# Strassen's products for the two-tile passes of a mixture-of-experts layer, and a second bank for the sums of its second matrix

## The chip, the cores and the metric

The kernel runs on one core of a Trainium2 chip, in fp32 throughout. The time is that of one execution on the device, in microseconds. In the profile PE is the engine of the matmuls, PEld its loading of weights, DVE the vector engine, ACT the scalar engine, POOL the GpSimd engine and SP the engine whose queue issues most of the DMAs.

## The reference

Two sequences of 1024 tokens of 512 numbers go through a feed-forward layer, an attention layer and a second feed-forward layer with the same weights, each added to its input. The attention (16 heads, with 64 memory slots and gates) isn't touched by the change. The feed-forward layer sends each token to one of two experts:

```python
logits = x_flat @ w_router.T
probs = softmax(logits); top_idx = argmax(probs); top_weight = probs[top_idx]
h = einsum('nd,ehd->enh', x_flat, w_fc)          # 512 -> 2048
a = square(where(h >= 0, h, 0.5 * h))
expert_out = einsum('enh,edh->end', a, w_proj)   # 2048 -> 512
out = einsum('end,en->nd', expert_out, mask * top_weight)
x = x + 0.5 * ffn(layernorm(x))
```

## The kernel before

A feed-forward layer (`ffn`, called once for each) sorts the tokens by expert and works them off in six passes; a pass is one, two or four tiles of 128 tokens that all go through one expert. The first layer's passes (FIRST) have 2, 4, 2, 4, 1 and 4 tiles, the last layer's (LAST) 4, 4, 4, 2, 2 and 1. Pass 0 of the first layer is cut up to begin while tokens still arrive. A pass takes the 2048 hidden units in four chunks (`ck`) of 512. Each chunk needs 1 MB of the first matrix (wfc) and 1 MB of the second (wp), loaded on SP's queue into a ring of 11 large buffers. "Pass 2_1" below means pass 2, chunk 1.

*Plain chunks* (passes of one and two tiles): `hidden` (L514) multiplies, four matmuls for each of four blocks of 128 hidden units, with all tokens of the pass as moving columns (128 or 256). `activate` (L496) does the leaky square: ACT takes a scaled ReLU of the product in PSUM (L500), DVE combines it with the product in PSUM (L501), ACT squares. `project` (L733) multiplies by wp, four matmuls of 512 columns for each tile, and its sums stay in PSUM over the four chunks; after the last one DVE scales them by the router's weight and adds the input (L740), and `send` (L653) scatters the tile with an indirect DMA on POOL's queue.

*Fast chunks* (passes of four tiles): both matrix products are done as Strassen's, in Winograd's form, with seven products of half-sized blocks in place of eight.

- Sums of blocks come first. Of the tokens: `token_sums`, four DVE operations for each pass (L538-544). Of the weights: `weight_sums` (S, L553-557) and `output_sums` (R, L567-571), eight POOL operations for each chunk, into a ring of six buffers (`sums`). Of the activations: `unit_sums` (Q, L588-591), eight DVE operations for each chunk.
- `hidden_fast` (L598-645) runs twice in a chunk (q = 0, 1), with 14 matmuls each (L611) into three banks, hU, hV and hC. DVE and ACT put the products together into hA and hB in SBUF: hA from hC (L627), hB from hV (L636), ACT copies (L618, L639), hA from hV (L643). hV gets its second product only after hB has been taken from its first. `activate` then reads hA and hB in SBUF (L503), and ACT squares.
- `project_fast` (L664) runs its products between the hidden matmuls of the next chunk, three at each step. Three of the seven (`keep`) gather in banks of their own over the four chunks; the other four (`add`) go through a bank of tag "at", of which `keep` leaves one free, and are added into osum in SBUF, by ACT in chunk 0 (L692) and by DVE after it (L694).
- `finish_fast` (L706-723) puts the output blocks together on DVE in the next pass's chunk 0, scales them (L721) and sends the tiles.

`prepare` (L476-493) normalises the next pass's tokens on DVE (xn, L481) and transposes them on PE through the bank "tr" (`lt`, L487). All engines take their instructions in program order, and so do the queues of SP and POOL.

The attention's weights need such sums too. `Attention.weight_sums` (L858-905) makes those of head group 0 in 12 steps: a load of 1 MB on SP (L179, L884), four POOL operations of 128x512 (L863-869), three stores on SP (L873-875), and so on for three blocks. The top level (L1421) runs these steps in chunk 2 of pass 2 of the first layer, three at each step of `ffn`.

Of the kernel before, what the change touches and what calls it, by code (L numbers as in the profile page):

```python
# [15 lines left out]
P = 128  # L16
# [33 lines left out]
def tile_macaron(  # L50
# [406 lines left out]
    def ffn(m, views):  # L457
# [15 lines left out]
            weight[ps] = mw  # L473


        def prepare(ps, raw):  # L476
            n = PASSES[ps]
            xT = ready[ps] = large_tile([P, DC, n * P], f"xsT{ph}_{ps}")
            for j in range(n):
                xn = work.tile([P, D], F32, tag="og", name=f"xn{ph}_{ps}_{j}")  # L480
                nc.vector.tensor_scalar(  # L481
                    xn, raw[:, j, 0:D], raw[:, j, D : D + 1], raw[:, j, D + 1 : D + 2],
                    ALU.subtract, ALU.mult,
                )
                tp = ps1.tile([P, DC, P], F32, tag="tr", name=f"lt{ph}_{ps}_{j}")
                for dc in range(DC):
                    nc.tensor.transpose(tp[:, dc, :], xn[:, ts(dc, P)], ident)  # L487
                nc.scalar.copy(xT[:, :, ts(j, P)], tp)
                yield
            if n == 4:  # L490
                yield from token_sums(ps, xT)


# [37 lines left out]


        def token_sums(ps, xT):
            lo, hi = slice(0, 256), slice(256, 512)
            T = sum_tile([P, 3, 2, 256], f"T{ph}_{ps}")
            b12 = xT[:, 0:2, hi]
            V = nc.vector
            V.tensor_tensor(T[:, 0], b12, xT[:, 0:2, lo], ALU.subtract)  # L538
            yield
            V.tensor_tensor(T[:, 1], xT[:, 2:4, hi], T[:, 0], ALU.subtract)  # L540
            yield
            V.tensor_tensor(b12, xT[:, 2:4, hi], b12, ALU.subtract)
            yield
            V.tensor_tensor(T[:, 2], xT[:, 2:4, lo], T[:, 1], ALU.subtract)
            ready[ps, "T"] = T[:, 0], T[:, 1], b12, T[:, 2]
# [28 lines left out]


        def unit_sums(ps, ck, q, a):
            nm = f"Q{ph}_{ps}_{ck}_{q}"
            if ck % 2 == 0:
                S = work.tile([P, 4, 256], F32, tag="qT", name=nm)
                S = [S[:, i, :] for i in range(4)]  # L580
            else:
                S = []
                for tag in A_TAGS[2 * q : 2 * q + 2]:
                    t = work.tile([P, 2, 256], F32, tag=tag, name=nm + tag, bufs=3)
                    S += [t[:, 0, :], t[:, 1, :]]
            lo, hi = slice(0, 256), slice(256, 512)
            V = nc.vector
            V.tensor_tensor(S[0], a[q][:, hi], a[q + 2][:, hi], ALU.add)  # L588
            V.tensor_tensor(S[1], S[0], a[q][:, lo], ALU.subtract)
            V.tensor_tensor(S[2], a[q][:, lo], a[q][:, hi], ALU.subtract)  # L590
            V.tensor_tensor(S[3], a[q + 2][:, lo], S[1], ALU.subtract)
            return S
# [4 lines left out]

        def hidden_fast(ps, ck, xT, T, wfc, S, a, sums):  # L598
            w = wfc.rearrange("p (k d h) -> p k d h", k=2, d=2)
            lo, hi = slice(0, 256), slice(256, 512)  # L600
            a += [None] * 4
            for q in range(2):
                nm = f"{ph}_{ps}_{ck}_{q}"
                first, second = ts(q, P), slice(256 + q * P, 256 + (q + 1) * P)
                U = ps2.tile([P, 256], F32, tag="pj", name=f"hU{nm}")
                V = ps2.tile([P, 256], F32, tag="pj", name=f"hV{nm}")
                C = ps1.tile([P, 256], F32, tag="st", name=f"hC{nm}")

                def product(bank, left, right, start):
                    for d in range(2):  # L610
                        m.mark = nc.tensor.matmul(  # L611
                            bank, lhsT=left[:, d, :], rhs=right[:, d, :],
                            start=start and d == 0, stop=d == 1, skip_group_check=True,
                        )

                def keep(name, bufs=2):
                    t = work.tile([P, 256], F32, tag=name, name=f"{name}{nm}", bufs=bufs)
                    nc.scalar.copy(t, U)  # L618
                    return t

                hA = work.tile([P, 512], F32, tag="oT", name=f"hA{nm}")
                hB = work.tile([P, 512], F32, tag="oT", name=f"hB{nm}")
                product(U, w[:, 0, :, first], xT[:, 0:2, lo], True)
                p1 = keep(("kp", "kv")[q], 1)
                product(V, S[0][:, :, first], T[0], True)
                product(C, w[:, 1, :, first], xT[:, 2:4, lo], True)
                added = nc.vector.tensor_tensor(hA[:, lo], C, p1, ALU.add)  # L627
                with tc.issue_after(added.ins):
                    flush()
                yield  # L630
                product(U, S[1][:, :, first], T[1], False)
                u2 = keep("e")
                yield
                product(U, S[2][:, :, first], T[2], False)
                u3 = keep("uT")
                nc.vector.tensor_tensor(hB[:, hi], V, u3, ALU.add)  # L636
                yield
                product(U, w[:, 1, :, second], T[3], False)
                nc.scalar.copy(hB[:, lo], U)  # L639
                a[q + 2] = activate(hB, q + 2, nm + "b")  # L640
                yield
                product(V, S[3][:, :, first], xT[:, 2:4, hi], False)
                nc.vector.tensor_tensor(hA[:, hi], V, u2, ALU.add)  # L643
                a[q] = activate(hA, q, nm + "a")
                late.append(lambda q=q: sums.append(unit_sums(ps, ck, q, a)))
# [17 lines left out]

        def project_fast(ps, ck, a, S, wp, R, p, raw):  # L664
            w = wp.rearrange("p (k q d) -> p k q d", k=2, q=2)
            lo, hi = slice(0, 256), slice(256, 512)
            nm = f"{ph}_{ps}_{ck}"
            if ck == 0:
                for i, (pool, tag) in enumerate(OP_TAGS[1:]):
                    p[i] = pool.tile([P, 2, 256], F32, tag=tag, name=f"o{i}_{nm}")  # L670
                p["sum"] = large_tile([P, 4, 2, 256], f"osum_{nm}")
            acc = p["sum"]


            def product(bank, left, right, first, last):
                for t in range(2):
                    for q in range(2):
                        nc.tensor.matmul(  # L678
                            bank[:, t, :], lhsT=left(q)[:, ts(t, P)], rhs=right(q),
# [6 lines left out]
                yield from product(p[i], left, right, ck == 0, ck == NHQ - 1)  # L686

            def add(i, left, right):
                bank = ps2.tile([P, 2, 256], F32, tag="at", name=f"oa{i}_{nm}")
                yield from product(bank, left, right, True, True)  # L690
                if ck == 0:
                    nc.scalar.copy(acc[:, i], bank)  # L692
                else:
                    nc.vector.tensor_tensor(acc[:, i], bank, acc[:, i], ALU.add)  # L694

            yield from add(0, lambda q: a[q][:, lo], lambda q: w[:, 0, q, lo])
            yield from keep(0, lambda q: a[q + 2][:, lo], lambda q: w[:, 1, q, lo])
            yield from add(1, lambda q: S[q][1], lambda q: R[1][:, q, :])
            yield from keep(1, lambda q: S[q][3], lambda q: w[:, 1, q, hi])
            yield from add(2, lambda q: S[q][2], lambda q: R[2][:, q, :])  # L700
            yield from keep(2, lambda q: a[q + 2][:, hi], lambda q: R[3][:, q, :])
            yield from add(3, lambda q: S[q][0], lambda q: R[0][:, q, :])


        def finish_fast(ps, p, raw):
            V, acc = nc.vector, p["sum"]  # L706
            u3 = work.tile([P, 2, 256], F32, tag="th", name=f"ou3{ph}_{ps}")
            V.tensor_tensor(acc[:, 1], acc[:, 0], acc[:, 1], ALU.add)
            V.tensor_tensor(acc[:, 0], p[0], acc[:, 0], ALU.add)
            V.tensor_tensor(u3, acc[:, 1], acc[:, 2], ALU.add)  # L710
# [3 lines left out]
            V.tensor_tensor(acc[:, 1], acc[:, 1], acc[:, 3], ALU.add)  # L714
            yield
            V.tensor_tensor(acc[:, 3], u3, acc[:, 3], ALU.add)
            for j in range(4):
                yield
                y = raw[:, j, 0:D].rearrange("p (c d) -> p c d", c=2)
                i = 2 * (j // 2)  # L720
                V.scalar_tensor_tensor(  # L721
                    y, acc[:, i : i + 2, j % 2, :], weight[ps][:, j : j + 1], y,
                    ALU.mult, ALU.add,
                )
                send(ps, j, raw)
# [23 lines left out]
        pending = ending = None  # L749
        late = []  # L750
        for ps in range(NPASS):
            fast = PASSES[ps] == 4
            ops = {} if fast else []
            for ck in range(NHQ):
                if ps == 0 and ck == 0:
# [58 lines left out]
                for _ in ending or ():  # L814
                    pass
                ending = None
                if ck == 0 and ps and PASSES[ps - 1] == 4:
                    ending = finish_fast(ps - 1, *before)
                    next(ending)
                if fast:  # L820
# [589 lines left out]
    for ps, ck in ffn(first_mixture, x1_views):  # L1410
# [7 lines left out]
                for load in (att.load_values_gates, att.load_keys_slots, att.load_queries, att.load_outputs):  # L1418
                    load(0, 0)

        if ps == 2 and ck == 2:  # L1421
            for _ in range(min(3, 12 - done)):
                next(weight_steps)
                done += 1
    for _ in norm:
        pass
    last_steps = ffn(last_mixture, out_views)
# [48 lines left out]
```

## Time and profile before

| | |
|---|---|
| time, median of 3 | 2299.93 us (2298.08 to 2301.12) |
| profiled execution: time, span, granted clock | 2298.89 us, 2297.2 us, 0.997 |
| PE busy | 2223.4 us, 97% |
| DVE busy | 1359.5 us, 59% |
| POOL busy | 471.5 us, 21% |
| FIRST pass 2 (181.4 to 248.7 us) | 67.3 us: PE 62.9, DVE 31.4, POOL 29.0 |
| FIRST pass 4 (345.3 to 384.0) | 38.7 us: PE 38.7, POOL 12.1 |
| LAST pass 3 (2136.5 to 2197.8) | 61.3 us: PE 61.3, DVE 19.8, POOL 3.9 |
| LAST pass 4 (2197.8 to 2253.3) | 55.5 us: PE 55.5, DVE 8.8, POOL 1.9 |

In rows of a timeline the first number is the start in microseconds after the span's start, the second the duration; then engine, line, operation, out<-in, partitions x elements and the count of instructions in the row. What stands in brackets is the idle time of the engine before it and what ended it. The stages above are cut by PE's work; each also holds the last projection of the pass before.

### The profile page before, as it was taken

To read this page: it belongs to the slowest core of one execution; us is meant where nothing else is said; L and a number is where in the kernel's file an instruction comes from. 1 tells how busy PE (TensorE), PEld (TensorE's weight loads), DVE (VectorE), ACT (ScalarE), POOL (GpSimd) and SP (SyncE) were. 2 spreads that over 40 slices of the span, in tenths; PEclk is the share of its full clock that TensorE was granted. 3 is DMA by queue.
4 is the path that set the end of the run, shared out by engine and by line. 5 is a ranking of instruction groups with operands and counts; after the bars stand their busy time and mean duration, and the time that the engine had idled before them with its cause. 6 is when DMAs were issued, how large, how long until landed. Compare 5 with 4: busy or idle time off the path is not lost.

```text
span 2297.2 us, 28881 instructions
## 1 busy us (share of the span) xinstructions
PE 2223.4 (97%) x10776; PEld 1532.2 (67%) x10776; DVE 1359.5 (59%) x3124; ACT 779.2 (34%) x1526; POOL 471.5 (21%) x400
## 2 busy tenths in 40 slices
PE   6999999999999999999999999999999999999998
PEld 5687687876556666655666656656655677888765
DVE  6544545666556656666865755755656767675411
ACT  2222222224334343434443443433344332222222
POOL 3523615301101101100101000000001435444000
PEclk9999999999999999999999999999999999999999
DMA  8515525241321311310312110210110313322442
GB/s 293 226 55 205 193 74 224 97 143 37 105 75 56 133 47 65 112 63 28 129 51 74 61 46 19 74 33 19 55 38 1 111 42 138 133 83 97 170 174 101
DMA packets 56940, 222.75 MB, mean 97 GB/s; under 512 B 5983, under 2 KB 13151, under 8 KB 38880
## 3 DMA queue, kind: packets, MB, share of 16 engines
q1 hardware_dynamic: 51232, 203.52, 25.1%
q0 software_dynamic: 5280, 16.85, 1.9%
q8 instruction: 86, 1.41, 0.2%
q10 hardware_dynamic: 288, 0.52, 0.1%
q14 instruction: 54, 0.44, 0.1%
HBM read 189.86 MB, written 31.54 MB: 96 GB/s over the span
## 4 chain that ended last, share of the span: by engine, by line
PE 74%; DVE 14%; issue 6%; POOL 2%; ACT 2%; DMA 1%; SPq 0%; POOLq 0%; DVEq 0%; ACTq 0%
PE U L954 9%; PE po L954 7%; PE oa L678 6%; PE kU L954 6%; PE hU L611 5%; PE V L954 5%; PE o L678 5%; PE pq L954 4%; PE hp L514 4%; PE hV L611 3%; PE op L733 3%; PE C L954 2%; PE svp L954 2%; PE AB L954 2%; PE ok L954 2%
## 5 line engine op out<-in xcount | busy, mean ns | idle before, releaser
L1251 POOL TENSOR_TENSOR sg<-sg,ms 128x512 f32<-128x512 f32 x64 | 68.7, 1073 | 1148.0 <-DVE ms L1249 1080.8
L954 PE MATMUL po<-wo,oT 128*128 128x512 f32 x512 | 230.3, 592 | 0.0
L954 PEld LDWEIGHTS po<-wo,oT 128*128 128x128 f32 x512 | 94.8, 190 | 93.7 <-issue 91.8
L514 PE MATMUL hp<-xsT,wfc 128*128 128x256 f32 (+1 forms) x768 | 147.7, 346 | 9.0 <-DVE t L501 4.6
L514 PEld LDWEIGHTS hp<-xsT,wfc 128*128 128x128 f32 x768 | 126.3, 190 | 32.1 <-issue 10.9
L733 PE MATMUL op<-wp,a 128*128 128x512 f32 x320 | 143.2, 593 | 0.0
L1247 ACT ACT_TABLE_LOAD x63 | 80.8, 1283 | 146.8 <-DVE ms L1246 137.9
L501 DVE SCALAR_TENSOR_TENSOR t<-hp,r 128x256 f32<-128x256 f32 (+1 forms) x96 | 36.4, 379 | 152.2 <-ACT r L500 149.2
L954 PE MATMUL U<-vgT,X 128*128 128x512 f32 x256 | 120.3, 592 | 0.0
L1147 DVE RECIPROCAL rC<-CT 128x256 f32<-128x256 f32 x64 | 112.2, 1753 | 2.2
L954 PE MATMUL pq<-xnT,wq 128*128 128x512 f32 x256 | 113.0, 592 | 0.0
L954 PE MATMUL kU<-ksT,X 128*128 128x256 f32 x384 | 102.2, 389 | 1.1 <-DVE E L1047 0.6
L611 PE MATMUL hU<-xsT,wfc 128*128 128x256 f32 x384 | 100.5, 384 | 0.5 <-ACT e L618 0.5
L733 PEld LDWEIGHTS op<-wp,a 128*128 128x128 f32 x320 | 59.7, 190 | 60.9 <-issue 57.4
L1177 DVE TENSOR_REDUCE mx<-ts 128x4 f32<-128x256 f32 x64 | 27.0, 422 | 106.1 <-PE ts L954 105.9
L954 PEld LDWEIGHTS pq<-xnT,wq 128*128 128x128 f32 x256 | 48.3, 190 | 59.3 <-issue 58.1
L954 PEld LDWEIGHTS kU<-ksT,X 128*128 128x128 f32 x384 | 67.8, 190 | 27.1 <-issue 12.5
L500 ACT ACTIVATE r<-hp 128x256 f32<-128x256 f32 (+1 forms) x96 | 33.3, 348 | 151.9 <-PE hp L514 147.6
L611 PEld LDWEIGHTS hU<-xsT,wfc 128*128 128x128 f32 x384 | 73.0, 193 | 14.1 <-issue 3.5
L1180 ACT ACT_TABLE_LOAD x63 | 80.8, 1283 | 1.1
L954 PEld LDWEIGHTS U<-vgT,X 128*128 128x128 f32 x256 | 48.6, 190 | 47.5 <-issue 45.9
L1098 ACT COPY kET<-tk 128x512 f32<-128x512 f32 x64 | 37.5, 586 | 125.3 <-PE tk L954 125.2
(301 smaller groups left out, 5071.4 us busy)
## 6 DMA issues: line engine op xcount, KB each, us to landing
wfc<-in_w_fc_dram SPq DMA_DIRECT2D x48, 1024.0 KB, 5.4
wp<-in_w_proj_dram SPq DMA_DIRECT2D x48, 1024.0 KB, 7.0
vgT<-vgs SPq DMA_DIRECT2D x16, 1024.0 KB, 5.2
wv<-in_w_v_dram SPq DMA_DIRECT2D x8, 1024.0 KB, 5.2
ksT<-kss SPq DMA_DIRECT2D x8, 1024.0 KB, 4.7
wo<-in_w_o_dram SPq DMA_DIRECT2D x8, 1024.0 KB, 4.8
xs<-xs SPq DMA_DIRECT2D x6, 1032.0 KB, 5.1
wks<-in_w_ks_dram SPq DMA_DIRECT2D x24, 256.0 KB, 2.8
```

The costliest lines, as they stand in the source:

```text
L500: nc.scalar.activation(r, h, AF.Relu, scale=0.5)
L501: m.mark_dve = nc.vector.scalar_tensor_tensor(t, h, 0.5, r, ALU.mult, ALU.add)
L514: m.mark = nc.tensor.matmul(hp, lhsT=wfc[:, dc * HQ + hc * P : dc * HQ + (hc + 1) * P], rhs=xT[:, dc, :], start=(dc == 0), stop=(dc == DC ...
L611: m.mark = nc.tensor.matmul(bank, lhsT=left[:, d, :], rhs=right[:, d, :], start=start and d == 0, stop=d == 1, skip_group_check=True,)
L678: nc.tensor.matmul(bank[:, t, :], lhsT=left(q)[:, ts(t, P)], rhs=right(q), start=first and q == 0 and (t == 0 or last), stop=last and q == ...
L733: nc.tensor.matmul(ops[j], lhsT=a[hc][:, ts(j, P)], rhs=wp[:, ts(hc, D)], start=(ck == 0 and hc == 0), stop=(ck == NHQ - 1 and hc == HQ // ...
L954: att.pe = op(*args, **kw)
L1098: nc.scalar.copy(u.kET, tp)
L1147: nc.vector.reciprocal(u.rC, u.CT)
L1180: nc.scalar.activation(u.u, u.u, AF.Exp)
L1247: nc.scalar.activation(ms, ms, AF.Sqrt, bias=eps, scale=1.0 / DV)
L1251: u.gated = then.gated = nc.gpsimd.tensor_tensor(sg, sg, ms.to_broadcast([P, HG, DV]), ALU.mult)
```

## The change

Three things change. Passes of two tiles, except pass 0 of the first layer, take the fast way: FIRST's pass 2 and LAST's passes 3 and 4, twelve chunks. Their blocks are half as wide on the side of the tokens (128 columns in the first product; in the second, one tile in place of two), the sums of weights are as large as before. Then `add` takes its bank by turns from "at" and from "tr", in all fast passes. And the twelve steps for the attention's weights move to pass 4 of the first layer (one tile), one at each step of `ffn`. The lines of the changed kernel lie 9 to 13 further on: the first product is L620, the second L689, the unit sums L597-600, the activation L510 (PSUM) and L512 (SBUF), osum L705 (ACT) and L707 (DVE).

```diff
@@ ffn @@
+        def is_fast(ps):
+            return PASSES[ps] > 1 and not (ps == 0 and m.split)
+
+        def token_halves(ps):
+            n = PASSES[ps] * P // 2
+            return slice(0, n), slice(n, 2 * n), n
@@ prepare @@
-            if n == 4:
+            if is_fast(ps):
                 yield from token_sums(ps, xT)
@@ token_sums; unit_sums and hidden_fast change in the same way @@
-            lo, hi = slice(0, 256), slice(256, 512)
-            T = sum_tile([P, 3, 2, 256], f"T{ph}_{ps}")
+            lo, hi, n = token_halves(ps)
+            T = sum_tile([P, 3, 2, n], f"T{ph}_{ps}")
...
@@ project_fast @@
-            lo, hi = slice(0, 256), slice(256, 512)
+            w_lo, w_hi = slice(0, 256), slice(256, 512)
+            lo, hi, n = token_halves(ps)
+            n //= P
...
-                p["sum"] = large_tile([P, 4, 2, 256], f"osum_{nm}")
+                p["sum"] = large_tile([P, 4, n, 256], f"osum_{nm}")
...
-                for t in range(2):
+                for t in range(n):
...
             def add(i, left, right):
-                bank = ps2.tile([P, 2, 256], F32, tag="at", name=f"oa{i}_{nm}")
+
+                pool, tag = ((ps2, "at"), (ps1, "tr"))[i % 2]
+                bank = pool.tile([P, n, 256], F32, tag=tag, name=f"oa{i}_{nm}")
                 yield from product(bank, left, right, True, True)
...
@@ finish_fast @@
-            V, acc = nc.vector, p["sum"]
-            u3 = work.tile([P, 2, 256], F32, tag="th", name=f"ou3{ph}_{ps}")
+            V, acc, n = nc.vector, p["sum"], PASSES[ps] // 2
+            u3 = work.tile([P, n, 256], F32, tag="th", name=f"ou3{ph}_{ps}")
...
-            for j in range(4):
+            for j in range(2 * n):
                 yield
                 y = raw[:, j, 0:D].rearrange("p (c d) -> p c d", c=2)
-                i = 2 * (j // 2)
+                i = 2 * (j // n)
                 V.scalar_tensor_tensor(
-                    y, acc[:, i : i + 2, j % 2, :], weight[ps][:, j : j + 1], y,
+                    y, acc[:, i : i + 2, j % n, :], weight[ps][:, j : j + 1], y,
                     ALU.mult, ALU.add,
                 )
                 send(ps, j, raw)
@@ the loop over passes @@
-            fast = PASSES[ps] == 4
+            fast = is_fast(ps)
...
-                if ck == 0 and ps and PASSES[ps - 1] == 4:
+                if ck == 0 and ps and is_fast(ps - 1):
                     ending = finish_fast(ps - 1, *before)
@@ the program's top level, first layer @@
-        if ps == 2 and ck == 2:
-            for _ in range(min(3, 12 - done)):
-                next(weight_steps)
-                done += 1
+        if ps == 4 and done < 12:
+            next(weight_steps)
+            done += 1
```

## The prediction

> **What bounds the kernel now.** The page was read from the top: span, engines, chain. Then the waits of PE, then the timelines of PE, DVE and POOL in the passes that the change touches.
>
> ```profile
> span 2297.2 us, 28881 instructions
> PE 2223.4 (97%) x10776; PEld 1532.2 (67%) x10776; DVE 1359.5 (59%) x3124; ACT 779.2 (34%) x1526; POOL 471.5 (21%) x400
> PE 74%; DVE 14%; issue 6%; POOL 2%; ACT 2%; DMA 1%; SPq 0%; POOLq 0%; DVEq 0%; ACTq 0%
> ```
>
> PE is busy for all but 73.8 us of the span, and the chain is mostly PE's: fewer matmuls shorten the program, if nothing else becomes late. POOL's 21% is an average over stages; in the feed-forward passes it is the engine to watch.
>
> The groups of PE's waits (in total, times, longest) give what can be won beside the matmuls:
>
> ```profile
> PE oa L678 <- DVE osum L694: 9.4, 8, 2.2
> PE hV L611 <- DVE hB L636: 7.3, 5, 2.9
> PE hp L514 <- DVE t L501: 4.6, 3, 1.9
> PE hp L514 <- DMA wfc<-in_w_fc_dram: 2.6, 2, 1.5
> ```
>
> PE's timeline in pass 2 of the first layer (two tiles), and then in a one-tile pass of the last layer; the starts of consecutive rows give the spacing of matmuls (a matmul is two records):
>
> ```profile
> 205.86 1.99 PE L514 MATMUL hp<-xsT,wfc 128*128 128x256 f32 x8 [1.87 <-DVE t L501]
> 209.21 1.99 PE L514 MATMUL hp<-xsT,wfc 128*128 128x256 f32 x8 [1.35 <-DVE t L501]
> 211.04 7.03 PE L733 MATMUL op<-wp,a 128*128 128x512 f32 x16
> 217.90 7.07 PE L514 MATMUL hp<-xsT,wfc 128*128 128x256 f32 x32
> 224.81 7.03 PE L733 MATMUL op<-wp,a 128*128 128x512 f32 x16
> ...
> 2253.31 3.86 PE L514 MATMUL hp<-xsT,wfc 128*128 128x128 f32 x32
> 2257.01 5.32 PE L733 MATMUL op<-wp,a 128*128 128x512 f32 x12
> ```
>
> (217.90 − 211.04)/8 = 0.858 us for 512 columns, (224.81 − 217.90)/16 = 0.432 for 256, (2257.01 − 2253.31)/16 = 0.231 for 128. The small form loses little.
>
> Now what two engines do to each other. DVE, first free in the first layer, then beside POOL's weight sums in a four-tile pass of the last; then POOL in the second stretch:
>
> ```profile
> 159.53 0.42 DVE L588 TENSOR_TENSOR Q<-a_1a,a_1b 128x256 f32<-128x256 f32 x1
> 159.86 0.42 DVE L590 TENSOR_TENSOR Q<-a_1a 128x256 f32<-128x256 f32 x1
> ...
> 1937.47 1.48 DVE L590 TENSOR_TENSOR Q_1msk<-a_1a 128x256 f32<-128x256 f32 x1
> 1938.88 1.48 DVE L589 TENSOR_TENSOR Q_1sg<-Q_1sg,a_1a 128x256 f32<-128x256 f32 x1
> 1940.40 1.38 DVE L591 TENSOR_TENSOR Q_1msk<-a_1b,Q_1sg 128x256 f32<-128x256 f32 x1
> 1941.70 0.68 DVE L694 TENSOR_TENSOR osum<-oa,osum 128x512 f32<-128x512 f32 x1
> ...
> 1937.35 1.33 POOL L554 TENSOR_TENSOR S<-S,wfc 128x512 f32<-128x512 f32 x1
> 1938.64 1.45 POOL L556 TENSOR_TENSOR wfc<-wfc 128x512 f32<-128x512 f32 x1
> 1940.05 1.45 POOL L557 TENSOR_TENSOR S<-wfc,S 128x512 f32<-128x512 f32 x1
> ```
>
> A unit sum takes 0.42 us alone and 1.38 to 1.48 beside a POOL sum: it ends when the POOL operation ends (1938.88+1.48 = 1940.36; POOL's 1938.64+1.45 = 1940.09), and the two step on in turn, some 1.4 us a step. The osum at 1941.70, one of whose operands is in PSUM, takes its usual 0.68 although POOL is at work. So DVE operations that have only SBUF operands wait for POOL; those that read PSUM do not.
>
> **The change part by part.**
>
> *Matmuls.* A plain two-tile chunk is 16×0.432 + 8×0.858 = 13.77 us. A fast one is 28 of 128 columns and 14 of 256: 28×0.231 + 14×0.432 = 12.52. Three passes (FIRST 2; LAST 3 and 4) of four chunks: 12×1.25 = −15.0 us, all on the path.
>
> *Alternating banks.* The 9.4 us of waits for osum come from each `add` needing the one free bank "at". With two banks a sum is read while the next is filled. The second bank "tr" is also that of the transposes in `prepare`, which can now wait for an osum (0.69 us). I take −8 (−9.4 to −3).
>
> *The weight sums leave FIRST pass 2.* Its stalls are 1.87 + 1.35 (DVE's finish of pass 1 ran beside the K sums on POOL, each L721 then 1.5 to 1.75 us instead of 0.74, with the activation queued behind it) and 1.14 for wfc, whose issue stood on SP behind the stores L873-875. −4.4 (−4.4 to 0: POOL's new sums can hold the same DVE work).
>
> *The same steps in pass 4.* The move takes along three loads of 1 MB and nine stores (3 MB): 6.3 MB. The stage of pass 4 (345.3 to 384) is 38.7 us, PE busy throughout, the DMA share 0.67 at 247 GB/s, so 12.8 us of transfer time are free; 6.3 MB at 430 GB/s (its busiest slices) need 14.7. POOL does 12 sums of 1.27 us (15.2) there, ahead of the sums for pass 5, and SP's stores hold wfc of 4_2, 4_3 and 5_0 behind POOL. Pass 5 has four tiles, 25.9 us a chunk, so what slips into it is covered. +1.5 (0 to 6).
>
> *DVE and POOL in fast two-tile chunks.* A plain chunk has four DVE operations, each reading PSUM: POOL cannot touch them. A fast chunk has 12 on SBUF (8 unit sums of 128x128, 4 activations of 128x256) and 10 on PSUM (6 of 128x128, 4 osum of 128x256). The L501 rows give 0.29 for 128x128 and 0.42 for 128x256: 8×0.29 + 4×0.42 + 6×0.29 + 4×0.42 = 7.4 us alone. POOL adds eight operations for each chunk (96 in all); the means of their groups sum to 11.4 us, which was 44% of a four-tile chunk of 25.9 and is 91% of 12.5. Sums for a chunk are made during the chunk before it, since the slots they go into come free only then: that is four chunks of FIRST (2_0 to 2_3) and seven of LAST (3_0 to 4_2). Each SBUF operation that meets POOL costs about 1.4 instead of 0.3 us.
> Lower bound, as if DVE never waited for PE: within 11.4 us of POOL, DVE gets through 6.7 SBUF operations (1.43 each) and 5.6 on PSUM (0.33); the remaining ten take 3.2 us: 14.6 against 12.5, +2.1 a chunk. Upper bound from the order on PE: between the end of hC and the second use of hV in the second half of a chunk lie three projection matmuls and eight hidden ones, 3×0.432 + 8×0.231 = 3.1 us; in it DVE must do hA, four unit sums, an osum and hB: 2.2 us free, 0.29 + 4×1.4 + 0.7 = 6.6 beside POOL, a stall of 3.5; the first half, with 0.9 us of slack and one activation plus three unit sums, adds about 1.5: +5.0. Four-tile chunks survived this because their window is 6.5 us. I take +3, as a stalled chunk also stretches and leaves POOL idle for part of it: 11×3 = +33 (23 to 55).
>
> *Finishes.* Those of the four-tile passes 1 (FIRST) and 2 (LAST), 7 sums and 4 scalings (7.8 us of DVE), ran beside plain chunks and now run beside fast ones; pass 3's (LAST), 4.5 us, replaces two scalings of 0.75. I take 3 + 3 + 2 = +8 (0 to 20). Token sums and normalisations in 2_3 and 3_3: +3 (0 to 8).
>
> Sum: −15.0 − 8 − 4.4 + 1.5 + 33 + 8 + 3 = +18.1 on the profiled execution's 2298.89, so 2317.0; this lies 1.0 below the median shown, and I state 2317. With costs at their least it is −4.4 (2294).
>
> The page "SBUF — State Buffer", section "SBUF: two separate sides", says that DVE and GpSimd share a port pair taken as an exclusive lock by whichever starts first, for the whole instruction; "Who interferes with whom" adds that a DVE operation with two SBUF inputs meets it and one with at most one does not. It speaks against this change, as the rows do; but by it POOL too would wait out DVE in full (1.27 + 0.42 = 1.69 a step, where the rows show 1.4). An estimate from that rule, port time 8×1.27 + 8×0.29 + 4×0.42 = 14.2 us a chunk, gives 11×1.7 = 18.7 us in place of 33, and a time of 2303.
>
> **The rivals.** (1) *Cover holds, faster.* DVE has 5 us of room in a chunk (12.5 − 7.4), and in four-tile passes nearly half the unit sums already run beside POOL (L590 means 0.60 to 1.04 us), with only 10.4 us of hV waits in 24 chunks. If the SBUF operations fall where POOL waits for its slots, chunks cost nothing more: −15 − 8 − 4.4 = −27, 2272. It decides below 1.4 us lost a chunk ((27.4 − 12.5)/11), where the change breaks even. The 3.1 us window speaks against it. (2) *Partial cover*, 1 us a chunk and half the finishes: −27.4 + 11 + 7 = −9, 2290. (3) *POOL itself is late*: in 2_0 and 3_0 it also has four sends of about 1.0 us, 11.4 + 4.2 = 15.6 against 12.5, and PE waits for S: +3.1 twice and about 1 in 4_0 above my sum, 2324. (4) *Transfers of pass 4* overflow by the full 6 us: 2321. Weight loads as the bound are out: they are 190 ns in their rows, yet 128-column records come every 0.116.
>
> **How the numbers follow.** Contention on the path (the forecast, with 3 and 4 as its upper part) 0.66, own range 2300 to 2348; partial cover 0.20, 2285 to 2303; full cover 0.10, 2268 to 2285; worse than all of it 0.04. The range 2283 to 2343 leaves out most of the full cover, the worst, and the top of the first. 0.2% is 4.6 us, about what a measurement can tell: faster 0.27, same 0.08, slower 0.65.
>
> **What would show it.** Right: L597-600 and L512 in the two-tile passes at means near 1 us; PE waits hV <- hB and oa <- a or Q of 2 to 5 us a chunk in 3_0 to 4_2; stages of those passes longer than before (61.3 and 55.5 us) in spite of less PE work; waits for osum nearly gone; pass 4 of FIRST without DMA waits. Wrong: two-tile stages of 50 to 52 us, with the unit sums at 0.3 us; or PE waiting for S and R on POOL.

## The result, and the profile after

The changed kernel takes 2314.96 us (median of 4, 2313.45 to 2316.05), the kernel before 2299.63 beside it: ratio 1.0065, 95% interval 1.0052 to 1.0078. It is slower by 15.3 us, where 17 were forecast. The profiled execution took 2314.28 us, its span is 2312.6.

The head of the page and the chain of the changed kernel:

```profile
span 2312.6 us, 30271 instructions
PE 2223.6 (96%) x11208; PEld 1565.3 (68%) x11208; DVE 1489.0 (64%) x3361; ACT 789.5 (34%) x1586; POOL 603.1 (26%) x496
PE 73%; DVE 16%; issue 4%; DMA 2%; ACT 2%; POOL 1%; SPq 1%; another core or an unknown queue 0%; POOLq 0%; DVEq 0%; ACTq 0%
```

PE's busy time is that of before (2223.4), although its matmuls should have become shorter. Part of the waiting is counted as busy: in the rows below two matmul records after a wait take 0.70 us where others take 0.60, and the same matmuls without POOL's sums, in a run below, are busy for 2215.0. So PE's total doesn't show the loss. DVE has 130 us more; the added operations of the chunks, at what they take alone, would make some 70 of it (12 times the 7.4 − 1.7 us of the prediction).

Of PE's waits (in total, times, longest) these are the ones that the change bears on most:

```profile
PE hV L620 <- DVE hB L645: 16.2, 12, 3.4
PE oa L689 <- ACT a_1a L514: 5.8, 10, 0.7
PE hp L523 <- DVE t L510: 4.8, 3, 2.9
PE kU L967 <- DVE E L1060: 4.7, 2, 3.3
PE oa L689 <- DVE Q L598: 4.2, 3, 2.3
```

The wait of oa for osum (9.4 before) is gone, and that of the transposes for an osum, which the second bank made possible, is 0.8 us, once. In its place stand waits for hB (7.3 before), for the activation and for the unit sums Q.

Where the time went, by stages from PE's timeline. Each runs from its first hidden product to that of the next, so that it holds the last projection of the pass before:

| stage | before | after | difference |
|---|---|---|---|
| start to FIRST pass 1 | 85.1 | 86.5 | +1.3 |
| FIRST pass 1 | 96.3 | 94.8 | −1.4 |
| FIRST passes 2 to 4 | 202.6 | 209.5 | +6.9 |
| FIRST pass 5 and the attention | 1423.9 | 1427.3 | +3.4 |
| LAST passes 0 to 2 | 328.7 | 323.1 | −5.5 |
| LAST passes 3 and 4 | 116.8 | 129.1 | +12.2 |
| LAST pass 5 | 43.9 | 42.3 | −1.6 |

The four-tile stages got shorter, the two-tile stages longer. In the third row, pass 2 went from 67.3 to 72.2, pass 3 from 96.6 to 93.1 and pass 4, of one tile, from 38.6 to 44.2. The first stage ends between 84.4 and 88.4 in the runs below, so its +1.3 says nothing. What a steady fast chunk looks like, in LAST's pass 3: first DVE, then POOL, then PE.

```profile
2194.50 0.79 DVE L597 TENSOR_TENSOR Q<-a_1a,a_1b 128x128 f32<-128x128 f32 x1 [0.28 <-ACT a_1a L514]
2195.21 1.36 DVE L599 TENSOR_TENSOR Q<-a_1a 128x128 f32<-128x128 f32 x1
2196.49 1.36 DVE L598 TENSOR_TENSOR Q<-Q,a_1a 128x128 f32<-128x128 f32 x1
2197.78 0.41 DVE L707 TENSOR_TENSOR osum<-oa,osum 128x256 f32<-128x256 f32 x1
2198.11 0.28 DVE L600 TENSOR_TENSOR Q<-a_1b,Q 128x128 f32<-128x128 f32 x1
...
2193.81 1.33 POOL L563 TENSOR_TENSOR S<-S,wfc 128x512 f32<-128x512 f32 x1
2195.10 1.32 POOL L565 TENSOR_TENSOR wfc<-wfc 128x512 f32<-128x512 f32 x1
2196.38 1.32 POOL L566 TENSOR_TENSOR S<-wfc,S 128x512 f32<-128x512 f32 x1
...
2197.91 0.70 PE L689 MATMUL oa<-R,Q 128*128 128x256 f32 x2 [0.99 <-DVE Q L598]
```

The first three unit sums each end 0.15 us after a POOL operation does (2196.49+1.36 = 2197.85, POOL's 2196.38+1.32 = 2197.70, and so on). Then POOL stops, and the fourth takes 0.28. PE's product with Q waits for the third. From one chunk's second hC to the next one's, chunk after chunk from 2171.00 to 2253.78, are 16.6 us in the mean of five, against 13.77 for a plain chunk.

The longest stall in the two-tile passes is in chunk 3 of FIRST's pass 2, where DVE also has the token sums (L551, L553) of the four-tile pass after it, again DVE, POOL, PE:

```profile
248.78 1.75 DVE L551 TENSOR_TENSOR xsT<-xsT 128x512 f32<-128x512 f32 x1
250.45 1.74 DVE L553 TENSOR_TENSOR T<-xsT,T 128x512 f32<-128x512 f32 x1
252.12 0.28 DVE L645 TENSOR_TENSOR hB<-hV,uT 128x128 f32<-128x128 f32 x1
...
249.94 1.70 POOL L580 TENSOR_TENSOR R<-wp,R 128x512 f32<-128x512 f32 x1
251.61 1.71 POOL L562 TENSOR_TENSOR S<-wfc 128x512 f32<-128x512 f32 x1
...
252.45 1.21 PE L620 MATMUL hV<-xsT,S 128*128 128x128 f32 x4 [3.40 <-DVE hB L645]
```

hB itself, from PSUM, takes 0.28; it is late because two token sums of 0.69 became 1.75 ahead of it in DVE's order.

### The profile page after: what moved, and what is told of

Its sections match the earlier page's. It is cut to its first block, busy times and chain, and to the rows that moved or that the text cites. A ratio compares the mean times of both kernels' runs of the same rounds, so it can differ in the third digit from the quotient of the medians.

```text
span 2312.6 us, 30271 instructions
## 1 busy us (share of the span) xinstructions
PE 2223.6 (96%) x11208; PEld 1565.3 (68%) x11208; DVE 1489.0 (64%) x3361; ACT 789.5 (34%) x1586; POOL 603.1 (26%) x496
## 4 chain that ended last, share of the span: by engine, by line
PE 73%; DVE 16%; issue 4%; DMA 2%; ACT 2%; POOL 1%; SPq 1%; another core or an unknown queue 0%; POOLq 0%; DVEq 0%; ACTq 0%
PE U L967 9%; PE oa L689 8%; PE hU L620 7%; PE po L967 7%; PE o L689 6%; PE kU L967 5%; PE V L967 5%; PE pq L967 4%; PE hV L620 4%; PE C L967 2%; PE svp L967 2%; PE AB L967 2%; PE hC L620 2%; PE ok L967 2%; PE ov L967 2%
## 5 line engine op out<-in xcount | busy, mean ns | idle before, releaser
L967 PEld LDWEIGHTS po<-wo,oT 128*128 128x128 f32 x512 | 94.8, 190 | 93.7 <-issue 91.8
L620 PE MATMUL hU<-xsT,wfc 128*128 128x256 f32 (+1 forms) x576 | 131.3, 350 | 0.6 <-ACT e L627 0.6
L620 PEld LDWEIGHTS hU<-xsT,wfc 128*128 128x128 f32 x576 | 99.3, 192 | 16.3 <-ACT e L627 3.0
L562 POOL TENSOR_TENSOR S<-wfc 128x512 f32<-128x512 f32 x36 | 48.0, 1333 | 130.7 <-DMA wfc<-in_w_fc_dram 53.8
L620 PE MATMUL hV<-xsT,S 128*128 128x256 f32 (+1 forms) x288 | 66.3, 353 | 16.2 <-DVE hB L645 16.2
L1135 DVE TENSOR_TENSOR B<-AB,causal 128x256 f32<-128x256 f32 x128 | 48.2, 418 | 51.6 <-PE AB L967 51.3
L707 DVE TENSOR_TENSOR osum<-oa,osum 128x512 f32<-128x512 f32 (+1 forms) x108 | 64.4, 597 | 23.8 <-PE oa L689 22.4
L576 POOL TENSOR_TENSOR R<-wp 128x512 f32<-128x512 f32 x36 | 51.4, 1429 | 84.8 <-PE hU L620 60.2
L1013 ACT ACTIVATE th<-sg 128x512 f32<-128x512 f32 x64 | 40.3, 630 | 97.2 <-DVE sg L1011 97.2
```

The costliest lines, as they stand in the source:

```text
L562: G.tensor_tensor(S[:, 0], a21, w[:, 1, :, hi], ALU.add)
L576: G.tensor_tensor(R[:, 0], b12, w[:, 0, :, lo], ALU.subtract)
L620: m.mark = nc.tensor.matmul(bank, lhsT=left[:, d, :], rhs=right[:, d, :], start=start and d == 0, stop=d == 1, skip_group_check=True,)
L967: att.pe = op(*args, **kw)
L1013: nc.scalar.activation(th, v.sg, AF.Tanh, scale=0.5)
L1135: nc.vector.tensor_tensor(m[:, ts(j, NPR), :], pp[j][:, i], causal[:, 0:NPR, :], ALU.mult)
```

## The experiments

The theory: DVE's operations on SBUF wait for POOL's sums, and in two-tile chunks that lies on PE's path. The rivals: the small products are slow by themselves; the moved steps cost it; POOL is late.

### One part alone: the banks

```diff
 # kernel before
-                bank = ps2.tile([P, 2, 256], F32, tag="at", name=f"oa{i}_{nm}")
+                pool, tag = ((ps2, "at"), (ps1, "tr"))[i % 2]
+                bank = pool.tile([P, 2, 256], F32, tag=tag, name=f"oa{i}_{nm}")
```

> The kernel before with only the two banks by turns; passes of two tiles stay plain and the attention's weight steps stay in pass 2. Theory (each part has its own price): the waits of oa for osum, 9.4 us before, go, and the four-tile stages shorten as they did in the changed kernel (first layer's pass 1 -1.4, pass 3 about -3.5, last layer's passes 0 to 2 -5.5); the step from the first layer to the attention loses up to 3 (E of the attention behind the finish of pass 5, 1.45 + 3.26 us of waits in the changed kernel). Sum -7, 2293 us (2289 to 2297). Rival (the second bank's other user, the transposes, makes new waits and eats it): 2299 or more.

Measured: 2292.49 us beside 2299.19 (ratio 0.9970, 0.9961 to 0.9980), −6.7. The waits for osum are gone; the wait of the attention's first keys for E is there with the same 4.7 us. As forecast, though a later run shows that the reason given for it was not the root.

### One part alone: the steps in pass 4

```diff
 # kernel before
-        if ps == 2 and ck == 2:
-            for _ in range(min(3, 12 - done)):
-                next(weight_steps)
-                done += 1
+        if ps == 4 and done < 12:
+            next(weight_steps)
+            done += 1
```

> The kernel before with only the weight steps moved to pass 4 of the first layer. Theory (the move costs in pass 4 what the changed kernel showed there, 44.2 us in place of 38.6): +5.6 in pass 4, -4.4 in pass 2, so 2301 us (2298 to 2304), with DVE's t late behind POOL and not a DMA as the wait. Rival (pass 4's loss in the changed kernel came from the two-tile passes, whose sums push POOL's and SP's work back): pass 4 stays at 38.6 to 40 and the time falls to about 2296.

Measured: 2297.87 (0.9996, 0.9986 to 1.0005): no difference that can be told, just under the range expected and above the rival's 2296. Pass 2 is 5.1 us shorter (67.3 to 62.2); passes 3 and 4 together are 4.1 longer (135.2 to 139.4). So the loss in pass 4 belongs to the move and not to the fast passes, and the gain in pass 2 pays for it.

What is lost in pass 4 shows in the changed kernel, as rows of DVE, POOL and PE:

```profile
350.05 1.48 DVE L598 TENSOR_TENSOR Q_1sg<-Q_1sg,a_1a 128x256 f32<-128x256 f32 x1
349.81 1.44 POOL L880 TENSOR_TENSOR kw<-kw 128x512 f32<-128x512 f32 x1
351.79 3.52 PE L523 MATMUL hp<-xsT,wfc 128*128 128x128 f32 x16 [2.87 <-DVE t L510]
```

The last unit sums of pass 3 stand ahead of pass 4's first t on DVE, and beside the sums for the attention they take 1.4 to 1.5 us each in place of 0.42: the same meeting of DVE and POOL, in another place.

### POOL's sums taken away, or replaced by writes

The changed kernel, in two-tile passes; both leave out the sums of the weights. In the first the products take blocks of the weights themselves (the same for wp):

```diff
+            if PASSES[ps] == 2:
+                yield
+                made["S"] = w[:, 0, :, hi], w[:, 1, :, hi], w[:, 0, :, lo], w[:, 1, :, lo]
+                yield
+                return
```

> The changed kernel without POOL's eight sums for each chunk of a two-tile pass: the products take blocks of the weights in place of sums (this part of the computation is left out), all else as in the changed kernel. Theory (DVE's operations on SBUF wait for POOL's): unit sums of 128x128 fall from means of 0.28 to 1.04 us to 0.29, the chunk from 15.6 to about 12.7, the last layer's passes 3 and 4 from 129 to about 109 us, pass 2 of the first layer by 8 to 10; total about 2287 us (2282 to 2293). Rival (the small products and their chain through ACT and DVE are slow by themselves): chunks stay over 15 us and the time within 5 us of the changed kernel, 2310 to 2315.

In the second, POOL fills the same buffers with constants (again the same for wp):

```diff
+            if PASSES[ps] == 2:
+                for i in (0, 0, 1, 1, 1):
+                    G.memset(S[:, i], 0.5)
+                yield
+                for i in (0, 1, 2, 2, 2):
+                    G.memset(S[:, i], 0.5)
...
```

> The changed kernel with POOL's eight sums of a chunk of a two-tile pass replaced by twenty memsets of the same buffers (values 0.5: this part of the computation is left out), about 0.52 us each, so that POOL is as busy and its buffers and waits are the same, but it only writes SBUF. Theory (the two engines contend where both read SBUF): as without the sums, 2282 to 2293 us, unit sums near 0.29 us. Rival 1 (any POOL work slows DVE): 2308 to 2318 us, unit sums near 1 us or half of that beside shorter operations. Rival 2 (POOL is late with its sums, contention or not): as the changed kernel, with PE waiting for POOL.

Measured: 2287.38 without sums and 2290.23 with memsets, beside 2299.19 (0.9952, 0.9936 to 0.9969; 0.9964, 0.9950 to 0.9978). LAST's passes 3 and 4 in each, as busy times of PE, PEld, DVE, ACT, POOL (with counts), granted clock, DMA share and GB/s. The changed kernel:

```profile
2141.20:2270.30 129.10, 115.39 (x718) 99.43 (x716) 102.52 (x199) 34.10 (x108) 84.30 (x64) 1.00 0.43 151
```

Without sums:

```profile
2128.00:2240.40 112.40, 112.14 (x717) 100.09 (x715) 64.35 (x199) 34.24 (x108) 6.70 (x6) 1.00 0.49 168
```

With memsets:

```profile
2133.50:2245.90 112.40, 112.11 (x717) 100.08 (x715) 64.42 (x199) 34.26 (x108) 73.95 (x149) 1.00 0.49 174
```

The same 199 DVE instructions take 102.5 us beside POOL's sums and 64.4 without them, and the stage loses 16.7 us with them: without them five chunks, from hC to hC, take 13.3 us in the mean (2157.44 to 2223.91) in place of 16.6. With memsets POOL is busy for 74 us, in the same ring of buffers and behind the same waits for their slots, and DVE and PE don't notice. So it is not POOL's lateness nor its being busy, but its operations that read SBUF. DVE and POOL in a stretch of the memset run:

```profile
2180.33 0.29 DVE L615 TENSOR_TENSOR Q<-a_1a,a_1b 128x128 f32<-128x128 f32 x1 [0.15 <-ACT a_1a L514]
2180.54 0.28 DVE L617 TENSOR_TENSOR Q<-a_1a 128x128 f32<-128x128 f32 x1
2180.74 0.28 DVE L616 TENSOR_TENSOR Q<-Q,a_1a 128x128 f32<-128x128 f32 x1
...
2178.88 1.93 POOL L564 MEMSET S<- 128x512 f32 x4 [3.98 <-PE hV L638]
2180.75 0.53 POOL L567 MEMSET S<- 128x512 f32 x1
```

This is also what the Trainium skill says: "SBUF — State Buffer", section "Who interferes with whom", has a DVE instruction with two SBUF inputs contend with a GpSimd instruction that reads SBUF and not with one that only writes it. The runs agree: DVE's 199 operations took 102.5 us beside the sums and 64.4 beside the memsets.

### The same sums on another engine

Nothing is left out; only two-tile passes:

```diff
 # changed kernel, weight_sums and output_sums
-            G = nc.gpsimd
+            G = nc.vector if PASSES[ps] == 2 else nc.gpsimd
```

> The changed kernel with the eight weight sums of a chunk of a two-tile pass on DVE in place of POOL; nothing is left out. Theory (it is the meeting of the two engines that costs): DVE takes 0.69 us for a sum where POOL takes 1.27 or more, so a chunk has 7.4 + 8x0.69 = 12.9 us of DVE work, none of it waiting for POOL; the unit sums of these passes near 0.3 us, the last layer's passes 3 and 4 at 112 to 122 us (129 in the changed kernel), total 2290 to 2306 us, below the changed kernel's 2315. Rival (work of sums as such makes DVE's chain late, whoever does it): 2312 us or more.

Measured: 2289.47 beside 2299.69 (0.9955, 0.9938 to 0.9971), 25 us less than the changed kernel for the same arithmetic, and just under the lower end. LAST's passes 3 and 4, columns as above:

```profile
2132.40:2244.70 112.30, 112.03 (x717) 99.47 (x715) 94.94 (x255) 34.75 (x108) 6.79 (x6) 1.00 0.50 174
```

DVE does 56 more operations than in the changed kernel and is busy for 7.6 us less. PE is as free as with no sums at all.

### The steps back in pass 2

```diff
 # changed kernel
-        if ps == 4 and done < 12:
-            next(weight_steps)
-            done += 1
+        if ps == 2 and ck == 2:
+            for _ in range(min(3, 12 - done)):
+                next(weight_steps)
+                done += 1
```

> The changed kernel with the attention's weight steps back in chunk 2 of pass 2 of the first layer. Theory (the steps' place matters little by itself, but 15 us of POOL sums and nine stores now stand ahead of the sums that the two-tile pass waits for): pass 2 gets longer by 5 to 15 us and pass 4 back to about 39 us; total 2315 to 2325 us. Rival (the steps in pass 4 are what the changed kernel loses there): pass 4 gives 5.6 us back, and the total falls to 2309 or less.

Measured: 2328.18 (1.0122, 1.0105 to 1.0139), 13 us more than the changed kernel and 3 above the upper end. From pass 2's first product to pass 3's are 85.0 us, against 72.2 in the changed kernel; pass 3 takes 98.3 against 93.1, and pass 4 is back at 38.6. PE's waits name the loads too, which SP issued only at 240.11 us, right behind the stores of the attention's sums:

```profile
PE hU L620 <- DMA wfc<-in_w_fc_dram: 5.9, 1, 5.9
```

So the move is right once pass 2 is fast, though it is worth nothing by itself.

### The change without its fast two-tile passes, and its boundary

The banks and the steps in pass 4 together (both diffs above):

> The kernel before with the banks by turns and the weight steps in pass 4: the change without its fast two-tile passes. Theory (the parts add up: -6.7 and -1.3 measured apart): 2291 us (2289 to 2293). Rival (they meet in pass 4): 2293 or more.

Measured: 2288.79 (0.9950, 0.9933 to 0.9966), −10.9, a little more than the two apart (−8.0) and just under the range. Hence the fast two-tile passes cost 26.2 us in the changed kernel (+15.3 against −10.9).

The steps in pass 3, and one bank in the first layer's last pass:

```diff
 # kernel before, with the banks by turns
-                pool, tag = ((ps2, "at"), (ps1, "tr"))[i % 2]
+                pool, tag = ((ps2, "at"), (ps1, "tr"))[0 if m.split and ps == NPASS - 1 else i % 2]
-        if ps == 2 and ck == 2:
-            for _ in range(min(3, 12 - done)):
-                next(weight_steps)
-                done += 1
+        if ps == 3 and done < 12:
+            next(weight_steps)
+            done += 1
```

> The kernel before with the banks by turns, except in the first layer's last pass, and the weight steps in pass 3 (four tiles). Theory (the 4.7 us of waits of the attention's first keys for E, behind the finish of pass 5, come from the order that the second bank gives there; and four-tile chunks of 25.9 us cover POOL's extra 15 us): 4 us less than with the banks alone in all passes, -4 for the stalls of pass 2 and little lost in pass 3; 2287 us (2284 to 2291). Rival (the steps' loads and sums hold the four-tile pass's own sums): 2292 or more.

Measured: 2287.91 (0.9944, 0.9927 to 0.9960), in the range, but only 0.9 below the run with the steps in pass 4, which is within the noise. The waits for E are down to those of the kernel before, and yet from pass 5's first product to the attention's first U are 121.1 us, as many as with two banks (121.4): without the second bank the rest of pass 5 must take longer by about what the boundary gains (one wait of 1.2 us for osum is back). So nothing was won back there.

### Fast passes in the last layer only, and then all sums on DVE

```diff
 # the run with two-tile sums on DVE
-            return PASSES[ps] > 1 and not (ps == 0 and m.split)
+            return PASSES[ps] > (2 if m.split else 1)
```

> Banks by turns, weight steps in pass 4, fast two-tile passes in the last layer only, their weight sums on DVE; the first layer's pass 2 plain again. Theory (with the meeting of the engines gone, a fast two-tile chunk saves 13.77 - 12.4 = 1.4 us in the last layer, while in the first layer's pass 2 its gain is lost in chunk 3 to DVE's normalisations and token sums for the four-tile pass after it): the last layer 4 us shorter than with plain passes, the first as with plain passes; 2285 us (2282 to 2287), below the 2289 of both kernels it is made from. Rival (their difference lies in the start and the boundary, not in the passes): 2288 to 2291.

```diff
 # the same, weight_sums and output_sums
-            G = nc.vector if PASSES[ps] == 2 else nc.gpsimd
+            G = nc.vector
```

> The same, with the weight sums of the four-tile passes on DVE too (eight operations of 0.69 us for each of 24 more chunks). Theory (the meeting of DVE and POOL also feeds the waits of hV for hB and hA in four-tile passes, some 10 us in the kernel before): DVE has 11.4 + 5.5 = 16.9 us of work in a chunk of 25.9, the unit sums of 128x256 fall from means of up to 1.3 us to 0.42, and the time falls by 3 to 6 more, to 2281 us (2278 to 2285). Rival (DVE now does the sums in the stretches where its chain is due, and POOL did them for nothing): 2286 us or more.

Measured: 2282.12 and 2270.69 beside 2297.89 (0.9932, 0.9919 to 0.9946; 0.9879, 0.9864 to 0.9894). Against before the first has −15.8, where plain two-tile passes gave −10.9 and fast ones in both layers −10.2: fast passes with their sums on DVE win 4.9 in the last layer and lose 5.6 in the first. (In the run with both, PE still waits 3.35 us for hB in the first layer's pass 2, behind the token sums, since POOL's sums for the four-tile pass after it run beside them; with all sums on DVE the changed kernel waits 0.6 us in all for hB.) The gain of 1.4 us a chunk that the expectation names was read too high: from hC to hC a chunk with its sums on DVE takes 12.8 to 13.3 us (14.1 where one pass gives way to the next), not 12.4, so that it gains 0.5 to 0.9. The second run gains 11.4 more, twice what was expected: the four-tile passes lost to POOL too.

### All sums on DVE, in the kernel before and in the changed one

In both kernels `weight_sums` and `output_sums` take `G = nc.vector` in place of `G = nc.gpsimd`.

> The kernel before with its weight sums (of the four-tile passes) on DVE in place of POOL, nothing else changed. Theory (the two engines' meeting already cost the kernel before, in its four-tile passes): as much off as the sums on DVE took off those passes between the last two runs, about -11 (2282.1 to 2270.7): 2287 us (2284 to 2291); waits of hV for hB and hA, 10.4 us before, nearly gone, those for osum partly. Rival (it only paid with the second bank): 2294 or more.

> The changed kernel with all weight sums of its feed-forward layers on DVE, pass 2 of the first layer fast as well. Theory: the run with all sums on DVE and a plain pass 2 in the first layer took 2270.7; a fast pass 2 gains up to 5 in its matmuls and loses about as much in chunk 3, where DVE has the next pass's normalisations and token sums: 2270 to 2276 us. Rival (without POOL in the four-tile passes either, the finish of pass 1 and the token sums fit): 2266 to 2269 us. In both, 40 us less than the changed kernel for the same arithmetic on another engine.

Measured, beside 2301.06: 2273.81 for the kernel before (0.9885, 0.9869 to 0.9902) and 2268.85 for the changed one (0.9867, 0.9850 to 0.9883). The kernel before gains 27 us, against 11 expected: this theory had the mechanism and less than half its size. LAST's passes 0 to 2 (four tiles), in the kernel before:

```profile
1807.80:2136.50 328.70, 314.11 (x1479) 264.38 (x1478) 215.97 (x429) 90.64 (x193) 141.51 (x107) 0.99 0.27 96
```

and with its sums on DVE:

```profile
1797.50:2111.00 313.50, 310.28 (x1478) 263.56 (x1477) 215.58 (x510) 90.90 (x193) 16.27 (x17) 1.00 0.29 101
```

DVE does 81 operations more in the same busy time, and PE's idle time falls from 14.6 to 3.2 us. Of PE's waits, over the whole of that kernel, those that were 7.3, 3.1 and 9.4 us in the kernel before:

```profile
PE hV L611 <- DVE hB L636: 1.1, 2, 0.6
PE hV L611 <- DVE hA L643: 0.3, 1, 0.3
PE oa L678 <- DVE osum L694: 0.2, 1, 0.2
```

The wait for osum, 9.4 us in the kernel before, is down to 0.2 with one bank. It came from DVE being late, not from the bank; the second bank only gave the lateness room. That is one reason why 11 was too little: it counted what sums on DVE bring after the banks had taken their part (6.7). The rest of the 27 lies in part in the first layer's pass 5: from its first product to the attention's first U are 114.6 us in place of 121.0, where the second bank had brought nothing (122.2 in the run with the banks alone).

The changed kernel with its sums on DVE came out as its rival had it (2266 to 2269), 5.0 us below the kernel before with its sums on DVE. The intervals of the two against the kernel before overlap, but each of its four runs (2264.98 to 2271.59) is below each of the other's four (2272.92 to 2275.09), and LAST's passes 3 and 4 take 112.1 us in place of 116.8. So without the meeting of the engines the change seems to pay, by about 5 us; four runs of each are few to give the size. Both are faster than either kernel of this case.

## Why the prediction was right

*The side and the size.* Forecast 2317, range 2283 to 2343, measured 2314.96. The step that decided it, "Each SBUF operation that meets POOL costs about 1.4 instead of 0.3 us", shows in the rows (1.36 against 0.28), and taking the meeting away in the two-tile passes takes 24 to 27 us off the changed kernel in three ways (memsets, sums on DVE, no sums; each against before).

*The steady chunk, +3.* Five chunks of the last layer's two passes lose 3.3 us each; the first two and the last, nothing. Seven times 3, finishes of 5 and a token term of 1 made 27 there, where 16.7 were measured. The place was right in part. The forecast set the stall "between the end of hC and the second use of hV", which is the wait for hB; of its 16.2 us in the changed kernel 11.3 lie in the two-tile passes. But in the last layer's two passes PE waited 4.8 us for hB, 4.9 for the unit sums and 2.7 for the activation, so that more than half of the waiting there stood in front of the projection. The number of chunks was too high, and the finishes cost nothing of their own in the last layer. Nor did every operation meet POOL: the 128x128 unit sums of these passes took 0.70 us in the mean, 21 of 60 over 1 us and 32 under 0.5, where the forecast's sign was "means near 1 us". The token sums cost more than their +3 in the first: the 3.40 us stall, and the slow clock after it (below).

*Matmuls, −15.0.* The durations were right, the sum was not reached. The same count gives 116.7 us for the last layer's passes 3 and 4 when plain (8×16×0.432 + 28×0.432 for the last projection of pass 2 + 56×0.858 + three tiles of transposes at 0.44), and 116.8 were measured; for fast passes it gives 107.5, and 112.4 were measured without sums on POOL. Pairs of 128-column products that wait for a bank follow each other by 0.55 us in place of 0.44, three times in a chunk (2185.14, 2186.27 and 2187.39 in that run), which is about half of the 4.9. The rest is pauses of 0.10 to 0.15 us, most of them before such a pair and too short for a row to show: the starts of PE's records in this stage have some 26 of them, about 3 us. So the stage gained 4.4 in place of the 9.2 of the count (10 for the eight chunks, whose last projection lies in the next stage).

These two errors go against each other: for the fast passes −15.0 + 44 = +29 was forecast, and +26.2 measured.

*The banks, −8.* Measured −6.7. The size held, the reason did not. The step said that the waits "come from each `add` needing the one free bank"; they vanish with one bank when the sums leave POOL. And the banks have a price that the forecast didn't name: the waits for E before the attention, 1.1 us before and 4.7 with them.

*The stalls of pass 2, −4.4, and the steps in pass 4, +1.5.* Measured −5.1 and +4.1. The second was mis-sized, inside its bounds (0 to 6): PE waits in pass 4 itself, for DVE's t (2.87 and 0.52 us in the changed kernel), which pass 5 can't cover, and after the longer wait its clock is low (0.53 from 351.4 to 355.0).

*The sum.* Forecast: −8 − 2.9 for banks and steps, +29 for the fast passes, +18.1. Measured: −10.9 and +26.2, +15.3. That the total is so near is partly luck: in the fast passes a saving too large met a cost too large, and the −10.9 is met to the tenth although its parts, measured apart, make −8.0.

*The rivals.* Full cover (2272) fell: POOL's sums and DVE's operations met in most chunks. Partial cover (2290) fell too: it had 1 us lost a chunk, and five of the last layer's lost 3.3 each. POOL late by itself (2324) fell with the memsets, and PE waited 0.3 us in all for S. Overflowing transfers (2321) fell: 0.8 us of waits for wfc in all; pass 4 did lose 5.6 us, but to DVE's late t. The estimate by the exclusive lock (2303) was too low: it gave 1.7 us a chunk, the time by which the two engines' work together overfills the chunk, and not what PE loses when its chain waits for single operations (3.3 in five chunks).

## What to carry to other kernels

Before work is added to a vector engine, look at whether its operations read SBUF while GpSimd's do: the same operation took 0.28 us or 1.36, and the kernel before took 27 us more than with its sums on DVE. An engine whose reads hold up the other's is not free help, however idle its line in the profile; in the two-tile passes, moving its work onto the "busier" engine made both less busy (DVE 102.5 to 94.9 us). And when a wait goes away with an extra buffer, ask whether the producer was late for another reason.

## What the hardware showed beside this

A long wait of PE can cost twice. At the first layer's end the changed kernel waits for E, and then:

```profile
509.66 2.08 PE L967 MATMUL kU<-ksT,xnT 128*128 128x256 f32 x4 [3.26 <-DVE E L1060]
...
512.38 3.35 PE L967 MATMUL U<-wv,xnT 128*128 128x512 f32 x4
515.57 1.88 PE L967 MATMUL C<-wv,xnT 128*128 128x512 f32 x4
```

The two last rows have four records of the same shape, which take 3.35 us and then 1.88; the granted clock is 0.57 from 511 to 516 and 1.00 after it. The same happens after the wait of 3.40 us at 252.45 (0.53 for 3.6 us), after that of 2.87 at 351.79 (0.53 for 3.6 us) and after one of 2.28 at 57.91 (0.51 for 3.4 us). After waits of 2.60 us at 216.06, 2.59 at 2176.10 and 2.28 at 2230.43 it does not (1.00). So in these rows the length of the wait alone does not decide it. The Trainium skill's "TensorE: Matmul & The Clock Gate", section "What's actually happening", gives an idle window of about 3.4 us after which the array runs at half its clock. The half clock agrees with the rows, and it lasts for one or two such windows; but it came after waits shorter than the window, and what decides is left open here. The prediction had not counted this cost, by estimate some 2 us each time (3.6 us at 0.53).
